# First layer of six experts by block products, turned rows copied by ScalarE, and one pool of banks, in a one-core graph and expert kernel

## The chip, the core and the metric

The kernel runs on one core of a Trainium2 chip. The metric is the device time of one execution in microseconds (us). Engines are named TensorE (PE in the profile; PEld is its weight loads), VectorE (DVE), ScalarE (ACT), GpSimd (POOL) and SyncE (SP). L1106 is line 1106 of the kernel before.

## The reference, cut to what matters

The input is 1250 rows (nodes) of 768 float32 values. A two-layer graph attention and a linear attention are added to it, and then a feed-forward part with eight experts, of which each row uses two:

```python
xt = layernorm(x)
scores, idx = top_k(xt @ Wg + bg, 2)
h = gelu(einsum('td,edh->eth', xt, W1) + b1[:, None, :])     # 768 -> 384, the first layer
y = einsum('eth,ehd->etd', h, W2) + b2[:, None, :]           # 384 -> 768, the second layer
out = x + sum over the two experts of a row of score * y
```

The kernel computes an expert only for rows that chose it. Everything is float32.

## The kernel before

The first part of the kernel (to about L1050) is the two attentions and, tile by tile of 125 rows, the norm and the routing: each tile's normalised rows and its eight gate values are written to a table in device memory, `xl_d` (L937 and L951), and a list `idx` of the rows that belong to each expert is built on VectorE with small products on TensorE (L958 to L1049). The last two of ten tiles are routed at 842 to 866 us.

Then the experts run. Each has three fixed tiles of 128 rows (`FIX`), and rows beyond that go to extra tiles (`other`, L1116), of which here one runs among the last expert's. For an expert:

- `gather` (L1060): three indirect loads on GpSimd's queue fetch rows by `idx` into `xg` (L1065, three buffers). Six transposes a tile on TensorE (L1074, "turns", into `px`) and two copies a tile on VectorE (L1075) make `xsT`, the turned rows: 768 values as 6 chunks of 128 partitions, by 384 rows. The gate values are copied at L1078.
- `inner` (L1081), the first layer: three blocks of 128 hidden values, each a sum of 6 products over the chunks (L1090, `ph`, 384 columns). ScalarE makes Gelu of each into `hT` (L1092). A float32 product runs as two passes, each counted as an instruction by the profile.
- `give` (L1095), for each of the three tiles: `gb`, the second bias by the gate value, on ScalarE (L1099); six products of 384 columns (L1106, `py`, two halves); `ys`, the result by the gate value plus `gb`, on VectorE (L1108, two halves, two buffers for three tiles); and a scatter that adds `ys` to rows of `out` from GpSimd's queue (L1110). Each scatter waits for the one before it, since both add to `out`.

The loop over experts 0 to 6 (L1160 to L1179) makes `inner` of expert e, `gather` of expert e+1, then the three `give` of expert e, and then issues from SyncE the second bias of expert e+2 (L1175) and both weight matrices of expert e+4 (`expert`, L748 and L750, ring of four buffers of 128x4608). The last expert (L1181 on) goes tile by tile together with the extra tile. A scheduler decides the order of each engine's instructions from dependences; an engine carries its own out in order. The eight banks of PSUM are shared out as two for turns (`x_p`), two for the first layer (`h_p`) and four for the second (`y_p`, L1056 to L1058). The large arrays `xnT` and `kept` of the attention part are no longer used when the experts run.

Of the kernel before, what the change touches and what calls it, by code (L numbers as in the profile page):

```python
# [27 lines left out]
F32 = mybir.dt.float32  # L28
# [5 lines left out]
AF = mybir.ActivationFunctionType  # L34
ALU = mybir.AluOpType
AX = mybir.AxisListType
PSUM = bass.MemoryType.PSUM
# [3 lines left out]
KC = D // 128  # L41
H1, C1, H2, C2 = 4, 192, 2, 96
HEADS, DH = 12, 64
NE, FF = 8, 384
FC = FF // 128
# [9 lines left out]
FIX = 3  # L55
# [5 lines left out]
def row_bcast(ap, parts):  # L61

    n = 1
    for s in ap.shape:
        n *= s
    return bass.AP(tensor=ap.tensor, offset=ap.offset, ap=[[0, parts], [1, n]])


@with_exitstack
def gps_block(ctx: ExitStack, tc: tile.TileContext, x, src, dst, norm_g, norm_b, W1, a_src1, a_dst1,  # L70
              b1, W2, a_src2, a_dst2, b2, Wu, bu, Wq, bq, Wk, bk, Wv, bv, Wo, bo, Wg, bg, fW1, fb1,
              fW2, fb2, out):
    nc = tc.nc
# [19 lines left out]
    kept = keep.tile([128, NT * H1 * CG], F32)  # L93
# [33 lines left out]
    xnT = big.tile([128, KC, N], F32)  # L127
# [4 lines left out]
    def bank(pool=None, name="mm"):  # L132
        return (pool or mm_p).tile([128, 512], F32, name=name)
# [37 lines left out]
    rows = fl.tile([KC, 128], F32)  # L171
# [36 lines left out]
    with tc.tile_pool(name="eps", bufs=4, space=PSUM) as eps_p:  # L208
# [4 lines left out]
        for k in (1, 0):  # L213
            nc.vector.memset(ends[k][:, T:], float(NO_NODE))
            for r0, r1 in blocks128:
# [5 lines left out]
                got = nc.scalar.copy(ends[k][:, r0:r1], pe[:, :nr])  # L221
# [78 lines left out]
    with tc.If(nc.values_load(odd[0:1, 0:1], min_val=0, max_val=1) > 0), ExitStack() as es:  # L300
# [9 lines left out]
        with tc.For_i(0, N, PT) as d0:  # L310
# [14 lines left out]
            with tc.For_i(0, TP, CH) as g:  # L325
                for u in range(CH):
                    at = bass.ds(g + u, 1)
                    count(ends[0][:, at], ends[1][:, at], False, u == CH - 1)
            A = cnt.tile([PT, N], F32)
            for i, (a, b) in enumerate(ACH):  # L330
                nc.scalar.copy(A[:, a:b], acc[:, i, :b - a])
            for g0 in range(0, NT, 4):
                n = min(4, NT - g0)
# [38 lines left out]
    with tc.tile_pool(name="ma_p", bufs=2, space=PSUM) as ma_p:  # L372
# [34 lines left out]
        ahead = {}  # L407
# [126 lines left out]
    def least(ss, H):  # L534
# [12 lines left out]
        return lo  # L547

    def attend(ss, sd, lo, wp, rb, gather):

        def across(cols, name, bufs, bias=0.0):
# [42 lines left out]
    with tc.tile_pool(name="wp", bufs=3) as wp, tc.tile_pool(name="rb", bufs=1) as rb:  # L594
        with tc.tile_pool(name="ag_p1", bufs=1, space=PSUM) as ag_p:
            for hd in range(H1):
# [10 lines left out]
                v = ag[:, :, :2 * CG].rearrange("p a (b c) -> p a b c", b=2)  # L607
# [8 lines left out]
        at = 2 * (C2 + 1)  # L616
# [22 lines left out]
    for t in range(NT):  # L639
# [3 lines left out]
        for k in range(2):  # L643
            half = slice(k * 384, (k + 1) * 384)
            for w in (Wk_sb, Wv_sb):
                ps = bank()
                for c in range(KC):
                    nc.tensor.matmul(ps[:PT, :384], xnT[:, c, t * PT:(t + 1) * PT], w[:, c, half],  # L648
                                     start=c == 0, stop=c == KC - 1)
# [10 lines left out]
            ps = bank()  # L660
            for c in range(3):
                nc.tensor.matmul(ps[:, c * 129:(c + 1) * 129],  # L662
                                 ky[:, (3 * k + c) * 128:(3 * k + c + 1) * 128], va[:, 3 * k + c],
                                 start=c == 0, stop=c == 2, skip_group_check=True)
            acc = kvacc[:, 3 * k:3 * k + 3]
            got = ps[:, :387].rearrange("p (b c) -> p b c", b=3)
# [25 lines left out]
    q3 = KC // 2  # L692
# [29 lines left out]
    for c in range(KC):  # L722
        ps = bank()
# [5 lines left out]
    for c in range(KC):  # L729
        for k in range(2):  # L730
            half = slice(k * 384, (k + 1) * 384)
            ps = bank()
# [12 lines left out]
    def expert(w1, w2, b2, b):  # L745

        t = wt.tile([128, KC, D], F32, name="w", bufs=4).rearrange("p c f -> p (c f)")
        nc.sync.dma_start(t[:, :KC * FF].rearrange("p (c f) -> p c f", c=KC),  # L748
                          w1.rearrange("(c p) f -> p c f", p=128))
        nc.sync.dma_start(t[:, KC * FF:].rearrange("p (c d) -> p c d", c=FC),  # L750
                          w2.rearrange("(c p) d -> p c d", p=128))
        if b2 is not None:
            nc.sync.dma_start(b, row_bcast(b2, 128))
        return t, b
# [5 lines left out]
    ring = []  # L760
# [7 lines left out]
    with ExitStack() as rs:  # L768
# [28 lines left out]
        for k in range(2):  # L797
            half = slice(k * 384, (k + 1) * 384)
            ps = bank()
# [195 lines left out]
        ahead = query(0)  # L995
        for p in range(NT // 2):
# [10 lines left out]
            if p + 1 < NT // 2:  # L1007
                ahead = query(p + 1)
# [44 lines left out]

    mix.close()
    sp = ctx.enter_context(tc.tile_pool(name="sp", bufs=2))
    x_p = ctx.enter_context(tc.tile_pool(name="x_p", bufs=2, space=PSUM))  # L1056
    h_p = ctx.enter_context(tc.tile_pool(name="h_p", bufs=2, space=PSUM))
    y_p = ctx.enter_context(tc.tile_pool(name="y_p", bufs=4, space=PSUM))  # L1058

    def gather(rows, e):  # L1060

        got = []
        for r in rows:
            xg = sp.tile([128, D + NE], F32, name="xg", bufs=3)
            nc.gpsimd.indirect_dma_start(xg, None, xl_d, bass.IndirectOffsetOnAxis(r, 0))  # L1065
            got.append(xg)
        xT = sp.tile([128, KC, FIX * 128], F32, name="xsT")
        gates = sp.tile([128, FIX], F32, name="gates")
        for j, xg in enumerate(got):
            for a in range(2):  # L1070
                px = x_p.tile([128, 512], F32, name="px")
                for c in range(3):
                    o = (3 * a + c) * 128
                    nc.tensor.transpose(px[:, c * 128:(c + 1) * 128], xg[:, o:o + 128], ident)  # L1074
                nc.vector.tensor_copy(xT[:, 3 * a:3 * a + 3, j * 128:(j + 1) * 128],  # L1075
                                      px[:, :384].rearrange("p (b n) -> p b n", b=3))
            at = slice(D + e, D + e + 1) if isinstance(e, int) else bass.ds(e + D, 1)
            nc.vector.tensor_copy(gates[:, j:j + 1], xg[:, at])  # L1078
        return xT, gates

    def inner(w, xT, bias, a=0, b=FIX, hT=None):  # L1081

        if hT is None:
            hT = sp.tile([128, FC, FIX * 128], F32, name="hT")
        n = slice(a * 128, b * 128)
        for f in range(FC):
            ph = h_p.tile([128, 512], F32, name="ph")
            for c in range(KC):
                o = c * FF + f * 128
                nc.tensor.matmul(ph[:, n], w[0][:, o:o + 128], xT[:, c, n], start=c == 0,  # L1090
                                 stop=c == KC - 1)
            nc.scalar.activation(hT[:, f, n], ph[:, n], AF.Gelu, bias=bias[:, f])  # L1092
        return hT

    def give(w, hT, j, rows, gates):  # L1095

        w, wb = w
        gb = sp.tile([128, D], F32, name="gb")
        nc.scalar.mul(gb, wb, gates)  # L1099
        ys = sp.tile([128, D], F32, name="ys")  # L1100
        for k in range(2):
            half = slice(k * 384, (k + 1) * 384)
            py = y_p.tile([128, 512], F32, name="py")
            for f in range(FC):
                o = KC * FF + f * D + k * 384
                nc.tensor.matmul(py[:, :384], hT[:, f, j * 128:(j + 1) * 128], w[:, o:o + 384],  # L1106
                                 start=f == 0, stop=f == FC - 1)
            nc.vector.scalar_tensor_tensor(ys[:, half], py[:, :384], gates, gb[:, half],  # L1108
                                           op0=ALU.mult, op1=ALU.add)
        nc.gpsimd.indirect_dma_start(out, bass.IndirectOffsetOnAxis(rows, 0), ys, None,  # L1110
                                     compute_op=ALU.add)

    def fixed(e):
        return [idx[:, v:v + 1] for v in range(e * NJ, e * NJ + FIX)]

    def other(k):  # L1116

        ve = nc.values_load(v_row[0:1, bass.ds(k, 1)], min_val=0, max_val=NV,
                            engines=[mybir.EngineType.DVE])
        ee = nc.values_load(e_row[0:1, bass.ds(k, 1)], min_val=0, max_val=NE - 1,  # L1120
                            engines=[mybir.EngineType.DVE, mybir.EngineType.SP])
        rows = sp.tile([128, 1], I32, name="rows")
        nc.vector.tensor_copy(rows, idx[:, bass.ds(ve, 1)])
        bias = sp.tile([128, FC, 1], F32, name="bias")
        nc.vector.tensor_copy(bias, fb1T[:, :, bass.ds(ee, 1)])
        w = expert(fW1[bass.ds(ee, 1)].rearrange("o d f -> (o d) f"),
                   fW2[bass.ds(ee, 1)].rearrange("o d f -> (o d) f"), fb2[bass.ds(ee, 1)],
                   sp.tile([128, D], F32, name="wb", bufs=1))
        return ee, rows, bias, w

    ahead = gather(fixed(0), 0)
# [19 lines left out]
    for vals, add, row in ((place, float(NV), v_row), (which, 0.0, e_row)):  # L1151
        pick = fp.tile([128, NE], F32, name="pick", bufs=2)
        nc.vector.tensor_mul(pick, vals, mine)
        one = fp.tile([128, 1], F32, name="one", bufs=2)
        nc.vector.tensor_reduce(one, pick, AX.X, ALU.add)
        pr = h_p.tile([128, 512], F32, name="ph")
        nc.tensor.transpose(pr[:1, :128], one, ident)
        nc.vector.tensor_scalar(row, pr[:1, :128], add, None, op0=ALU.add)

    for e in range(NE - 1):  # L1160
        xT, gates = ahead
        bias = fb1T[:, :, e:e + 1]
        if e:
            hT = inner(ring[e], xT, bias)
        else:
            hT = inner(ring[e], xT, bias, 0, 1)
            inner(ring[e], xT, bias, 1, FIX, hT)
        ahead = gather(fixed(e + 1), e + 1)
        if e == NE - 2:
            ee, more_rows, more_bias, more_w = first  # L1170
            more_xT, more_gates = gather([more_rows], ee)
        for j, rows in enumerate(fixed(e)):
            give(ring[e], hT, j, rows, gates[:, j:j + 1])
        if e + 2 < NE:
            nc.sync.dma_start(spare[e % 2], row_bcast(fb2[e + 2], 128))  # L1175
        if e + 4 < NE:
            ring.append(expert(fW1[e + 4], fW2[e + 4], None, spare[e % 2]))
        elif e + 4 == NE:
            first = other(0)  # L1179

    e = NE - 1  # L1181
    xT, gates = ahead
    bias = fb1T[:, :, e:e + 1]
    hT = inner(ring[e], xT, bias, 0, 1)
# [8 lines left out]
    with tc.If(count > 1):  # L1193
        with tc.For_i(1, count, 1) as k:
            ee, rows, bias, w = other(k)
            xT, gates = gather([rows], ee)
# [33 lines left out]
```

## Time and profile before

| what | us |
|---|---|
| median of three runs (lowest, highest) | 1097.52 (1096.05, 1099.54) |
| profiled execution: its own time | 1097.82 |
| its span | 1096.1 |
| TensorE busy, share of span | 1031.0, 94% |
| VectorE busy | 705.8, 64% |
| ScalarE busy | 359.9, 33% |
| granted TensorE clock, mean | 0.986 |
| first layer's start, experts 1 to 6 | 901.27, 926.50, 951.72, 976.95, 1002.17, 1027.40 |
| first layer's start, expert 7 | 1054.31 |

The profile is of one execution. A row of the timeline has the start, the duration, the engine, the line, the operation, what it writes and reads, how often it stands there without a break, and in brackets how long the engine stood idle before it and what ended that. A TensorE matmul's end is modelled, so starts are the better measure of a stretch. "Idle before" does not tell of a cost by itself; it tells what an engine waited for.

### The profile page before, as it was taken

The numbers are of one execution on the slowest core, as the hardware profiler recorded it, in microseconds if no ns is written. First come the engines' busy times: TensorE is split into PE (matmuls) and PEld (weight loads), VectorE is DVE, ScalarE is ACT, GpSimd is POOL, SyncE is SP. The second block draws the span as 40 slices with busy tenths as digits, with TensorE's granted clock in tenths as the row PEclk, the third lists the DMA queues.
The fourth block names the chain that finished last, engine by engine and source line by source line (L and its number), as shares of the span: only waits on it lengthen the run. The fifth ranks groups of instructions, "written<-read, shape, count | busy, mean of one in ns | idle before, by whom it ended". The sixth has DMA issues, their size and how long they took to land.

```text
span 1096.1 us, 12392 instructions
## 1 busy us (share of the span) xinstructions
PE 1031.0 (94%) x4630; PEld 701.6 (64%) x4630; DVE 705.8 (64%) x1460; ACT 359.9 (33%) x548; POOL 78.8 (7%) x106
## 2 busy tenths in 40 slices
PE   6999999999999999988999999999999499999996
PEld 5876666587878879544555555656665376666674
DVE  7866684697897957769687958686855522222321
ACT  4612226372728373283833121112110111111121
POOL 2000000000000000000001000000000122223321
PEclk9999999999999999999999999999999699999998
DMA  5060000000000002000035002021144847777534
GB/s 161 29 211 19 29 15 1 1 1 1 1 1 1 1 1 87 1 0 1 15 142 153 1 15 71 20 65 43 58 153 132 274 116 221 213 213 203 116 58 59
DMA packets 35412, 79.51 MB, mean 73 GB/s; under 512 B 7078, under 2 KB 15416, under 8 KB 35348
## 3 DMA queue, kind: packets, MB, share of 16 engines
q1 hardware_dynamic: 29588, 58.90, 16.8%
q0 software_dynamic: 5760, 19.78, 8.5%
q8 instruction: 37, 0.61, 0.2%
q14 instruction: 27, 0.22, 0.1%
HBM read 60.33 MB, written 18.34 MB: 72 GB/s over the span
## 4 chain that ended last, share of the span: by engine, by line
PE 73%; DVE 20%; DMA 2%; ACT 1%; issue 1%; POOL 0%; DVEq 0%; POOLq 0%; ACTq 0%
PE s L863 19%; PE mm L648 9%; PE ph L1090 9%; PE py L1106 8%; PE mm L477 8%; DVE scr L569 6%; DVE w L589 5%; DVE w L590 5%; PE ag L602 3%; PE mm L924 2%; PE ag L624 2%; PE ec L398 2%; PE mm L452 2%; PE px L1074 2%; PE rb L558 1%; PE mm L662 1%
## 5 line engine op out<-in xcount | busy, mean ns | idle before, releaser
L602 PE MATMUL ag<-kept,w 125*125 125x198 f32 x800 | 137.5, 333 | 5.1 <-DVE w L590 4.8
L602 PEld LDWEIGHTS ag<-kept,w 125*125 125x125 f32 x800 | 133.5, 188 | 9.0 <-DVE w L590 9.0
L1106 PE MATMUL py<-w,hT 128*128 128x384 f32 x300 | 100.9, 486 | 0.0
L1090 PE MATMUL ph<-xsT,w 128*128 128x384 f32 (+2 forms) x432 | 99.9, 390 | 0.0
L589 DVE TENSOR_TENSOR w<-v,w 125x1250 f32<-125x1250 f32 x60 | 86.3, 1453 | 6.0 <-ACT w L587 5.4
L648 PE MATMUL mm<-Wv_sb,xnT 128*125 128x384 f32 x240 | 85.6, 489 | 4.8 <-DVE kvacc L668 4.8
L1090 PEld LDWEIGHTS ph<-xsT,w 128*128 128x128 f32 x432 | 68.9, 191 | 30.3
L569 DVE CUSTOM_DVE_ANT_0 scr<-ss_row,mask 125x1250 bf16<-125x1250 f32 x60 | 87.2, 1453 | 1.6 <-ACT ss_row L560 1.2
L477 PE MATMUL mm<-Wg,xnT 128*125 128x400 f32 x240 | 87.7, 505 | 0.2 <-ACT xnT L367 0.2
L590 DVE SCALAR_TENSOR_TENSOR w<-w,AT 125x1250 f32<-125x1250 f32 x60 | 86.4, 1454 | 0.4
L588 ACT ACTIVATE v<-dn_row,sl 125x1250 f32<-125x1250 f32 x60 | 79.3, 1333 | 17.4 <-DVE w L589 16.9
L648 PE MATMUL mm<-Wk_sb,xnT 128*125 128x384 f32 x240 | 85.0, 487 | 0.0
L1108 DVE SCALAR_TENSOR_TENSOR ys<-py,gates,gb 128x384 f32<-128x384 f32 x50 | 30.3, 616 | 79.3 <-PE py L1106 54.7
L1106 PEld LDWEIGHTS py<-w,hT 128*128 128x128 f32 x300 | 55.1, 190 | 33.1
L1075 DVE COPY xsT<-px 128x384 f32<-128x384 f32 x50 | 25.8, 552 | 73.3 <-PE px L1074 73.3
L648 PEld LDWEIGHTS mm<-Wv_sb,xnT 128*125 128x125 f32 x240 | 42.5, 187 | 31.4 <-DVE kvacc L668 6.9
L477 PEld LDWEIGHTS mm<-Wg,xnT 128*125 128x125 f32 x240 | 42.5, 188 | 26.5 <-ACT xnT L367 0.9
L1099 ACT ACTIVATE gb<-spare,gates 128x768 f32<-128x768 f32 x24 | 22.4, 935 | 112.4 <-DVE ys L1108 94.8
L587 ACT ACTIVATE w<-up_row,s 125x1250 f32<-125x1250 f32 x40 | 53.2, 1331 | 17.7 <-PE ag L602 17.6
L648 PEld LDWEIGHTS mm<-Wk_sb,xnT 128*125 128x125 f32 x240 | 42.0, 187 | 22.7 <-issue 1.8
L863 PE MATMUL s<-w,xnT 128*125 128x384 f32 x150 | 55.4, 489 | 0.0
L863 PE MATMUL s<-w 128*125 128x384 f32 x150 | 53.9, 491 | 0.0
(328 smaller groups left out, 1515.1 us busy)
## 6 DMA issues: line engine op xcount, KB each, us to landing
w<-in_L_ffn_W_dram SPq DMA_DIRECT2D x18, 1152.0 KB
xt<-in_x_dram SPq DMA_DIRECT2D x20, 336.0 KB
out_dram<-xt SPq DMA_DIRECT2D x10, 336.0 KB
xl_d<-xl SPq DMA_DIRECT2D x10, 336.0 KB
spare<-in_L_ffn_b_dram SPq DMA_DIRECT2D x8, 384.0 KB
W_sb<-in_L_gnn_W_dram SPq DMA_DIRECT2D x1, 2304.0 KB
Wk_sb<-in_L_mix_Wk_dram SPq DMA_DIRECT2D x1, 2304.0 KB
Wv_sb<-in_L_mix_Wv_dram SPq DMA_DIRECT2D x1, 2304.0 KB
```

The lines of the kernel that those rows point to most:

```text
L477: nc.tensor.matmul(ps[:PT, :2 * (CG + 2)], xnT[:, c, t * PT:(t + 1) * PT], Wg1[:, c, 2 * k:2 * k + 2].rearrange("p h c -> p (h c)"), start ...
L569: nc.vector.tensor_tensor_reduce(scr, ss_row, mask[:, t], 1.0, 0.0, ALU.mult, ALU.max, top[:, t:t + 1])
L587: nc.scalar.activation(w, up_row, AF.Exp, bias=ss[:, st:st + 1])
L588: nc.scalar.activation(v, dn_row, AF.Exp, bias=sl[:, st:st + 1])
L589: nc.vector.tensor_tensor(w, v, w, op=ALU.max)
L590: nc.vector.scalar_tensor_tensor(w, w, 2.0, AT[:, st, :N], op0=ALU.min, op1=ALU.mult)
L602: nc.tensor.matmul(ag[:, t // 2, o:o + CG], w[:, t * PT:(t + 1) * PT], gw[:, st, hd], start=st == 0 and t % 2 == 0, stop=st == NT - 1, ski ...
L648: nc.tensor.matmul(ps[:PT, :384], xnT[:, c, t * PT:(t + 1) * PT], w[:, c, half], start=c == 0, stop=c == KC - 1)
L863: nc.tensor.matmul(ps, left[:, c], right[:, c], start=start and c == 0, stop=c == n - 1, skip_group_check=True)
L1090: nc.tensor.matmul(ph[:, n], w[0][:, o:o + 128], xT[:, c, n], start=c == 0, stop=c == KC - 1)
L1106: nc.tensor.matmul(py[:, :384], hT[:, f, j * 128:(j + 1) * 128], w[:, o:o + 384], start=f == 0, stop=f == FC - 1)
L1108: nc.vector.scalar_tensor_tensor(ys[:, half], py[:, :384], gates, gb[:, half], op0=ALU.mult, op1=ALU.add)
```

## The change

The first layer of experts 1 to 6 is computed as a product of two block matrices. The weights of the first layer are seen as 3 blocks of hidden values by 2 halves of the 768 inputs, the rows as 2 halves by 3 tiles, and each block as 3 chunks of 128x128. Plain multiplication takes 3x2x3 = 18 products of blocks; the change forms 15 from sums of blocks and adds the results up into the nine blocks of 128x128 of `hT`.

- 11 sums of weight blocks and 11 sums of row blocks per expert (`WAYS`; each 128x384, `make`), on VectorE, kept in the unused `xnT` and `kept`. The weight sums of expert e+1 are put between the products of expert e (`between`); the row sums of expert e+1 follow its `gather`, ahead of the three `give` of expert e.
- 15 products (`PRODUCTS`) of 3 matmuls of 128x128 each, in ten banks, five products adding onto a bank that already holds an earlier one.
- Out of the banks into `hT`: nine writes by ScalarE (copies and negated copies) and sixteen additions or subtractions by VectorE. Then ScalarE makes Gelu over `hT` in place, three times 128x384.
- `gather` for experts 1 to 7 copies the turned rows with ScalarE in place of VectorE.
- All banks of the expert part come from one pool of eight.

Experts 0 and 7 and the extra tile keep the plain `inner`. The diff, cut to its core:

```diff
+PRODUCTS = (
+    ("6", None, 1, 1, (1, "="), (2, "=-")),
+    ("10", None, 2, 4, (1, "+"), (3, "=-"), (7, "=")),
+    ("12", None, "12", 5, (8, "="), (9, "=")),
+    ("4", None, 5, "4", (8, "-"), (5, "=-")),
+    ("9", None, "9", "9", (4, "=-"), (3, "-")),
+    ("14", "6", "14", "14", (4, "+")),
+    ("13", None, "13", 3, (3, "+"), (6, "=")),
+    ("7", "12", "7", "7", (2, "+")),
...
-    x_p = ctx.enter_context(tc.tile_pool(name="x_p", bufs=2, space=PSUM))
-    h_p = ctx.enter_context(tc.tile_pool(name="h_p", bufs=2, space=PSUM))
-    y_p = ctx.enter_context(tc.tile_pool(name="y_p", bufs=4, space=PSUM))
+    e_p = ctx.enter_context(tc.tile_pool(name="e_p", bufs=8, space=PSUM))
...
+            def make(name=name, a=a, sign=sign, b=b):
+                op = nc.vector.tensor_add if sign > 0 else nc.vector.tensor_sub
+                op(got[name], got[a], got[b])
...
+    def inner15(A, B, bias, between):
+        hT = sp.tile([128, FC, FIX * 128], F32, name="hT")
+        C = [hT[:, i, j * 128:(j + 1) * 128] for i in range(3) for j in range(3)]
+        banks = {}
+        for name, onto, a, b, *uses in PRODUCTS:
+            ps = banks[name] = banks[onto] if onto else bank()
+            for c in range(q3):
+                nc.tensor.matmul(ps[:, :128], A[a][:, c], B[b][:, c], start=c == 0 and not onto,
+                                 stop=c == q3 - 1, skip_group_check=True)
+            for to, how in uses:
+                to = C[to - 1]
+                if how == "=":
+                    nc.scalar.copy(to, ps[:, :128])
+                elif how == "=-":
+                    nc.scalar.mul(to, ps[:, :128], -1.0)
+                elif how == "+":
+                    nc.vector.tensor_add(to, to, ps[:, :128])
+                else:
+                    nc.vector.tensor_sub(to, to, ps[:, :128])
+            if between:
+                between.pop(0)()
+        while between:
+            between.pop(0)()
+        for f in range(FC):
+            nc.scalar.activation(hT[:, f], hT[:, f], AF.Gelu, bias=bias[:, f])
+        return hT
...
+        between = []
+        if 0 < e < NE - 2:
+            A, between = weight_sums(ring[e + 1], e + 1)
         if e:
-            hT = inner(ring[e], xT, bias)
+            hT = inner15(now, B, bias, between)
+            now = A
         else:
             hT = inner(ring[e], xT, bias, 0, 1)
             inner(ring[e], xT, bias, 1, FIX, hT)
-        ahead = gather(fixed(e + 1), e + 1)
+        ahead = gather(fixed(e + 1), e + 1, nc.scalar.copy)
+        todo = []
+        if e < NE - 2:
+            B, todo = token_sums(ahead[0])
+        if e == 0:
+            now, between = weight_sums(ring[1], 1)
+        for make in todo:
+            make()
```

The weights, the indirect loads and the scatters are the same in number and size.

## The prediction

> **What bounds the kernel now.** I read the engines' totals first (TensorE 94% of the span), then the busy time of each engine between the starts of one expert's first layer and the next one's, then the timeline of one such stretch. The change touches experts 1 to 6, and these stretches say which wait ends last there:
>
> ```profile
> core 0: us, PE busy (x) PEld busy (x) DVE busy (x) ACT busy (x) POOL busy (x), PEclk, DMA share, GB/s
> 901.27:926.50 25.23, 25.23 (x92) 15.48 (x91) 6.91 (x15) 4.55 (x6) 7.67 (x6) 1.00 0.76 204
> 926.50:951.72 25.22, 25.22 (x91) 15.46 (x91) 6.91 (x15) 4.54 (x6) 7.70 (x6) 1.00 0.77 204
> ```
>
> The first column is the length of the stretch, the second TensorE's busy time: they are the same. An expert lasts 25.23 us because TensorE never stops; VectorE is busy for 6.91 and ScalarE for 4.55. So TensorE's saving shows only until something else takes 25 us. Two chains are already near. The timeline of one stretch:
>
> ```profile
> 926.34 11.77 PE L1090 MATMUL ph<-xsT,w 128*128 128x384 f32 x36
> 927.01 1.14 DVE L1108 SCALAR_TENSOR_TENSOR ys<-py,gates,gb 128x384 f32<-128x384 f32 x2 [3.73 <-DMA out_dram<-ys,idx]
> 927.68 1.59 POOL L1110 DMA_INDIRECT out_dram<-ys,idx  x1 [6.37 <-DVE ys L1108]
> ...
> 937.36 1.55 POOL L1110 DMA_INDIRECT out_dram<-ys,idx  x1 [8.09 <-DMA out_dram<-ys,idx]
> 937.95 0.82 PE L1074 MATMUL px<-ident,xg 128*128 128x128 f32 x6
> ...
> 944.02 0.62 DVE L1108 SCALAR_TENSOR_TENSOR ys<-py,gates,gb 128x384 f32<-128x384 f32 x1 [1.32 <-PE py L1106]
> 944.92 1.61 POOL L1110 DMA_INDIRECT out_dram<-ys,idx  x1 [2.14 <-DVE ys L1108]
> ...
> 951.75 0.37 SPq L748 DMA_DIRECT2D w<-in_L_ffn_W_dram  x1
> ...
> 952.21 1.14 DVE L1108 SCALAR_TENSOR_TENSOR ys<-py,gates,gb 128x384 f32<-128x384 f32 x2 [3.70 <-DMA out_dram<-ys,idx]
> ```
>
> The third tile's ys (952.21) uses the first tile's buffer (two buffers), so it waits until the first tile's scatter has landed: from the end of ys 0 (944.64) to ys 2 it is 7.57 us. Today VectorE merely idles there. And the scatters run one at a time: issues at 919.70, 927.68, 937.36, 944.92, that is 7.98, 9.68 and 7.56 apart. The list of waits over five experts has both:
>
> ```profile
> POOL out_dram L1110 <- DMA out_dram<-ys,idx: 40.0, 5, 8.1
> DVE ys L1108 <- DMA out_dram<-ys,idx: 18.8, 5, 3.9
> ```
>
> **TensorE's side.** First layer: 36 passes of 384 columns (18 products, two passes each) take from 926.34 to 937.95, 11.61 us, 322 ns a pass. The new one has 15 products of three 128x128 matmuls, 90 passes of 128 columns. Such passes are in the tail:
>
> ```profile
> 1066.05 4.18 PE L1090 MATMUL ph<-xsT,w 128*128 128x128 f32 x36
> 1070.07 1.13 PE L1106 MATMUL py<-w,hT 128*128 128x384 f32 x3
> ```
>
> 36 of them in 4.02 us (start to start): 112 ns, a third of 322, so nothing is lost to the narrow shape. 90 x 0.1117 = 10.05; the saving is 1.56 us an expert, 9.4 for six. Turns (18) and second layer (36 passes) stay: 25.23 - 1.56 = 23.67.
>
> **VectorE's side.** It loses six copies of xsT (3 pairs of 1.02 = 3.1 us) and gets, per expert, 22 sums of 128x384 and 16 additions of 128x128 out of PSUM. The nearest sums in the trace are 128x375:
>
> ```profile
> 702.70 0.55 DVE L856 TENSOR_TENSOR xnT<-xnT 128x375 f32<-128x375 f32 x1
> 703.17 0.54 DVE L857 TENSOR_TENSOR w<-w,xnT 128x375 f32<-128x375 f32 x1
> ...
> 704.21 0.55 DVE L1036 TENSOR_TENSOR kept<-kept,s 125x384 f32<-125x384 f32 x1
> 704.67 0.54 DVE L855 TENSOR_TENSOR zS<-qT 128x375 f32<-128x375 f32 x1
> 705.13 0.55 DVE L1018 TENSOR_TENSOR xt<-xt,kept 125x384 f32<-125x384 f32 x1
> ```
>
> Busy 0.55, but starts only 0.47 apart when the next does not read the last one's result, and 0.57 when it does (703.17 to 703.74). 22 x 0.465 = 10.2, with three dependent pairs 10.5. For the additions no row exists: 64-element operations start 0.15 apart (851.53, 851.68), 384-element ones 0.47, so 128 elements lie between; interpolated 0.21, taken as 0.20: 16 x 0.20 = 3.2 (bounds 2.4 and 7.5). VectorE then needs 10.5 + 3.2 + ys 3.4 + gates 0.3 = 17.4 of 23.67 us: enough if it never had to wait. But it takes its instructions in order, and in the built order of the changed program the three ys do not stand together. ys 2 of an expert stands ahead of all additions of the next one's products; then come 16 additions with 11 weight sums between and behind them; then 11 token sums; then ys 0 of the next. So the wait of ys 2 for the scatter, in which VectorE had nothing else to do, is now in series with all of that. Queued behind it are the additions, and on ScalarE gb of that tile (0.94) waits for ys 2 in front of the copies that empty the banks; TensorE's eighth product accumulates onto the third's bank, which ScalarE reads behind that gb. TensorE stands there. The loop, ys 0 to ys 0:
>
> end of ys 0 to ys 2: 7.57 as now if nothing else loads the queues; weight loads (951.75) now begin inside it, and a scatter beside such loads took 9.68 until the next could go. I take 8.3 (7.57 to 9.7). ys 2: 1.14; gates 0.27; additions 3.2; 22 sums 10.5; waits of the additions for ScalarE: gb 0.94, a negated copy 0.37 (as the 128x128 Gelu) and two plain ones at 0.27 (a copy of that size out of PSUM, L726) make 1.85, less 0.9 that VectorE has to do meanwhile, and two more negated copies behind it 0.8, so 1.7; wait for the first copy of turned rows, 0.5 (0 to 1.5); ys 0: 1.14. Sum 26.75, against 25.23 now: **+1.52**. It holds for experts 2 to 5 (expert 1 has its successor's weight sums done beforehand, expert 6 has none to make): 4 x 1.52 = +6.1. Expert 1 follows TensorE, -1.56. For expert 6 the loop is 11 sums shorter, but now scatters and the extra tile's gather bound it (26.91 today): -0.6 (-1.6 to +0.9).
>
> **ScalarE** gets nine bank copies (9 x 0.27 to 0.37), six copies of turned rows (0.47 each) and three Gelus from SBUF (0.58 each, as now): about 10 us of 25, so it is no bound by throughput; what hides it is that slack, and its order costs what stands above. One pool of eight banks costs nothing while the readers keep up, and is in the 1.7 where they do not. On the queues of SP and POOL gathers, scatters and loads keep their order, but for one weight load (848.21) that now goes ahead of the two writes of out's rows beside it, which nothing waits for then.
>
> **Ahead of the loop.** In the built order all 22 weight sums of experts 1 and 2 stand on VectorE among the routing of the last two token tiles: 4 ahead of the first one's normalised rows (850.68), 10 between that and the second one's (857.92), 8 between that and idx:
>
> ```profile
> 863.25 0.22 DVE L1049 SCALAR_TENSOR_TENSOR idx<-inv,free 128x80 int32<-128x80 f32 x1
> 865.48 1.06 POOL L1065 DMA_INDIRECT xg<-xl_d,idx  x1 [280.31 <-DVE e_row L1158]
> 871.95 2.46 PE L1074 MATMUL px<-ident,xg 128*128 128x128 f32 x9 [7.01 <-DMA xg<-xl_d,idx]
> ```
>
> TensorE idles 7 us for these gathers, so a later idx delays everything. The first 4 fall into idle time (2.72 before 846.14, 1.55 before 850.35). Ten take 4.7, less idle time 1.14 and 0.90: +2.7. Eight take 3.8, less about 0.8 of short gaps in that dependent chain: +3.0. idx is +5.7; between it and the gather there were 2.0, of which 1.7 are slack: the gather starts +4.0 later. Expert 0's turns now all stand ahead of its products, +0.5; weight loads that have gone further by then give some 0.5 back. I take **+4.0** (2 to 5.5; with a weight load later than its sum, more).
>
> **Sum:** 4.0 - 1.6 + 6.1 - 0.6 = +7.9. The profiled execution took 1097.82 (span 1096.1), 0.3 over the median 1097.52; so **1106**. 0.3% (3.3 us) is about what a measurement of this kernel can tell from no change.
>
> [...]
>
> **Rivals.**
> (a) *TensorE stays the bound.* If additions and sums go closer together than in my rows and the scatter lands by 7.57, with the waits for ScalarE hidden, the loop falls to 23.7 or less: 6 x -1.56 = -9.4, with the shift ahead +4.0: 1092.4 (1088.4 if the routing hides the sums too). For it: VectorE's work is 17.4. Against it: the order. It decides below 23.7, 3.1 less than my sum. 0.13.
> (b) *The loop is lighter.* At 7.57 for the scatter, 0.17 for an addition and 0.9 for ScalarE it is 24.7: 4.0 - 1.6 - 2.1 - 0.6 = -0.3, with half the shift ahead hidden lower yet; 1095 to 1101, about 1097.5. 0.17.
> (c) *The main case*, loop 25.8 to 28: 1101 to 1112, at 1106. 0.60.
> (d) *TensorE's clock falls in the stalls.* After 7.01 us idle it was granted 0.50 (871.95 to 873.50) and three turns took 0.92 for 0.33. If four stalls of 3 us did the same to the 48 passes behind them (5.4 us), up to 4 x 3 to 5.4 more: about 1120. [...] 0.07.
> (e) *The change does not do what it says*: TensorE's instruction list of the changed program has 45 matmuls in each of the six, so only the time could fail to move: 1097.5. 0.03.
>
> The range 1092 to 1113 takes in (a) with its shift, (b) and (c), and leaves out (d) and the lowest of (a). Faster by over 0.3%: (a), 0.13. Within: (e) and most of (b), 0.15. Slower: the rest, 0.72.
>
> **What would show it.** After: periods of about 23.7 for expert 1 and 26.5 to 27 for 2 to 5, with a TensorE gap of about 3 us behind the seventh product, released by ScalarE's copy; ys 2 waiting for the scatter with the additions behind it; idx some 5 us later; clock 1.00 in the loop. Equal periods near 23.7 with TensorE always busy would make this wrong, as would additions 0.14 or 0.4 apart, or a scatter that lands in 6.

## The result, and the profile after

The changed kernel took 1108.71 us (median of 6; 1105.64 to 1114.04) against 1098.74 for the kernel before (6 runs): ratio 1.0092, 95% interval 1.0068 to 1.0116. It is slower by 10 us; the forecast was 1106, or +7.9. The profiled execution took 1113.38 (span 1111.6, granted clock 0.975), one of the longer ones. Part of its length is older than the change: the same ScalarE instruction of the attention part (L904 before; called the mark below) starts at 790.57 before and at 795.66 after, though the program up to there is the same. So 5.1 of its 15.5 us are this execution's own, and 10.4 are the change's.

The stretches between first layers of the changed kernel, as shown for before. Columns: stretch, its length, busy time of each engine, granted clock, DMA share, GB/s:

```profile
910.79:935.09 24.30, 23.89 (x145) 18.93 (x144) 17.36 (x47) 8.51 (x21) 8.81 (x6) 1.00 0.77 200
935.09:961.10 26.01, 23.89 (x145) 18.93 (x144) 17.36 (x47) 8.51 (x21) 8.23 (x6) 1.00 0.73 200
961.10:986.47 25.37, 23.89 (x145) 18.93 (x144) 17.38 (x47) 8.51 (x21) 9.22 (x6) 1.00 0.76 203
986.47:1012.12 25.65, 23.89 (x145) 18.93 (x144) 17.35 (x47) 8.51 (x21) 8.02 (x6) 1.00 0.76 200
1012.12:1037.62 25.50, 23.89 (x145) 18.93 (x144) 12.82 (x36) 8.73 (x21) 7.95 (x6) 1.00 0.81 225
1037.62:1069.62 32.00, 27.59 (x152) 21.23 (x151) 9.58 (x28) 8.73 (x21) 6.05 (x5) 0.89 0.36 60
```

TensorE now has less to do than the stretch is long: something else ends it. Against 25.23 the first is 0.9 shorter, the next four together 1.6 longer, and expert 6 (26.91 before) is 5.1 longer. Ahead of them 910.79 stands against 901.27: +9.5, of which 5.1 were there at the mark already; the change's part is +4.4. With 0.2 at the end, 4.4 - 0.9 + 1.6 + 5.1 + 0.2 = 10.4.

One turn of the loop in the changed kernel's timeline:

```profile
950.57 1.03 DVE L1100 TENSOR_TENSOR xnT<-xsT 128x384 f32<-128x384 f32 x2 [0.35 <-ACT xsT L1157]
...
955.73 2.32 DVE L1190 SCALAR_TENSOR_TENSOR ys<-ps,gates,gb 128x384 f32<-128x384 f32 x4
...
957.14 1.61 POOL L1192 DMA_INDIRECT out_dram<-ys,idx  x1 [2.85 <-DVE ys L1190]
...
964.55 1.14 DVE L1190 SCALAR_TENSOR_TENSOR ys<-ps,gates,gb 128x384 f32<-128x384 f32 x2 [6.50 <-DMA out_dram<-ys,idx]
...
965.79 0.94 ACT L1181 ACTIVATE gb<-spare,gates 128x768 f32<-128x768 f32 x1 [3.37 <-DVE ys L1190]
...
966.79 0.59 ACT L1127 COPY hT<-ps 128x128 f32<-128x128 f32 x3
...
967.43 0.94 PE L1122 MATMUL ps<-xnT 128*128 128x128 f32 x6 [1.48 <-ACT hT L1127]
...
972.89 2.13 PE L1156 MATMUL ps<-ident,xg 128*128 128x128 f32 x18
```

The chain is the forecast's: ys 0 ends (956.87), its scatter lands, ys 2 starts 7.68 later (964.55), gb waits for it, ScalarE's bank copies for gb, TensorE's eighth product for the copies. TensorE's stall was 2.12, 1.48, 1.76 and 1.61 in experts 2 to 5; about 3 was expected. The granted clock stayed at 1.00.

Expert 6 is where most was lost. All 24 turns now stand ahead of its second layer, and the last six need the extra tile's rows:

```profile
1048.59 2.13 PE L1156 MATMUL ps<-ident,xg 128*128 128x128 f32 x18
1054.47 1.51 PE L1156 MATMUL ps<-ident,xg 128*128 128x128 f32 x6 [3.75 <-DMA xg<-xl_d,rows]
1055.78 14.00 PE L1188 MATMUL ps<-w,hT 128*128 128x384 f32 x36
```

The first 3.5 us after that wait by granted clock (the last three figures are clock, DMA share and GB/s):

```profile
1054.47:1058.00 3.53, 3.53 (x10) 2.62 (x11) 1.11 (x2) 0.00 (x0) 0.00 (x0) 0.50 0.02 5
```

TensorE idles 3.75 us and comes back at a granted clock of 0.50; the second layer then takes 13.84 (1055.78 to 1069.62), against 11.61 in the loop (949.49 to 961.10). Before, the turns stood between pieces of the second layer, and the idle time for these rows was 0.83.

Ahead of the loop:

```profile
874.39 0.22 DVE L1075 SCALAR_TENSOR_TENSOR idx<-inv,free 128x80 int32<-128x80 f32 x1
875.65 1.06 POOL L1147 DMA_INDIRECT xg<-xl_d,idx  x1 [285.49 <-DVE one L1237]
879.97 4.54 PE L1156 MATMUL ps<-ident,xg 128*128 128x128 f32 x18 [5.98 <-DMA xg<-xl_d,idx]
```

Less the 5.1 of the mark, idx is 6.0 later than before (863.25), the gather 5.1 (865.48), the first turn 2.9 (871.95), expert 1's first layer 4.4.

### The profile page after: what moved, and what is told of

Read it like the earlier page. It is cut to its first block, busy times and chain, and to the rows that moved or that the text cites. A ratio compares the mean times of both kernels' runs of the same rounds, so it can differ in the third digit from the quotient of the medians.

```text
span 1111.6 us, 13347 instructions
## 1 busy us (share of the span) xinstructions
PE 1032.4 (93%) x4954; PEld 730.7 (66%) x4954; DVE 765.6 (69%) x1646; ACT 386.6 (35%) x644; POOL 82.8 (7%) x106
## 4 chain that ended last, share of the span: by engine, by line
PE 64%; DVE 24%; DMA 5%; ACT 3%; issue 1%; POOL 0%; DVEq 0%; POOLq 0%; ACTq 0%; SPq 0%
PE s L889 18%; PE mm L674 9%; PE mm L503 7%; DVE scr L595 6%; DVE w L615 5%; DVE w L616 5%; PE ps L1188 4%; DMA out_dram<-ys,idx 3%; PE ag L628 3%; PE mm L950 2%; PE ag L650 2%; PE ps L1172 2%; PE ps L1122 2%; PE mm L478 2%; PE ec L424 2%; DVE xnT L1100 2%
## 5 line engine op out<-in xcount | busy, mean ns | idle before, releaser
L1188 PE MATMUL ps<-w,hT 128*128 128x384 f32 x300 | 100.6, 494 | 0.0
L1188 PEld LDWEIGHTS ps<-w,hT 128*128 128x128 f32 x300 | 57.4, 194 | 38.3 <-issue 2.1
L1190 DVE SCALAR_TENSOR_TENSOR ys<-ps,gates,gb 128x384 f32<-128x384 f32 x50 | 29.1, 612 | 76.8 <-PE ps L1188 36.4
L431 DVE TENSOR_TENSOR AT<-AT,ec 125x120 f32 x162 | 44.6, 275 | 11.5 <-PE ec L424 8.7
L650 PE MATMUL ag<-w,h 125*97 125x417 f32 (+1 forms) x120 | 46.6, 531 | 4.8 <-DVE w L616 4.8
L1192 POOL DMA_INDIRECT out_dram<-ys,idx x24 | 40.2, 1677 | 133.6 <-DVE ys L1190 82.2
```

What stands on the lines that cost most here:

```text
L431: nc.vector.tensor_add(here, here, ec[:, g])
L650: nc.tensor.matmul(ag[:, i, :b - a], h2[:, st, hd * (C2 + 1):(hd + 1) * (C2 + 1)], w[:, a:b], start=st == 0, stop=st == NT - 1)
```

## The experiments

**Theory 1**: the loop passes through VectorE's queue because ys 2 waits there for the scatter, and a third buffer breaks it. **Rival 2**: the scatters among themselves are the loop (now 8.1, 8.9 and 8.4 us apart). **Rival 3**: VectorE has too many small operations. The other two losses, ahead of the loop and in expert 6, were tried by themselves. All ratios are against the kernel before, on the same chip. Differences in us from the changed kernel are between medians of separate measurements, in which the kernel before stood between 1097.5 and 1099.3; they are good to a us or two.

### A third buffer for ys

```diff
-        ys = sp.tile([128, D], F32, name="ys")
+        ys = sp.tile([128, D], F32, name="ys", bufs=3)
```

> The changed kernel with three buffers for ys in place of two; nothing else. In the changed kernel the first layers of experts 2 to 5 start 25.4 to 26.0 us apart. Theory 1 (VectorE's in-order queue is the bound, since ys of the third tile waits 7.7 us for the first tile's scatter with the next expert's additions queued behind it): the wait goes, TensorE's stall after the seventh product goes, and the four periods fall to 23.7 to 24.3, some 5 to 7 us in all. Rival 2 (the chain of scatters, each of which waits for the one before: 8.1, 8.9 and 8.4 us apart now, sum 25.4): the periods stay within 0.3 us of 25.4 and the stall moves to the next tile of ys. Rival 3 (VectorE's own work of 38 small operations): the periods stay above 25 with VectorE busy and no scatter in its waits.

1100.78 us, ratio 1.0024 (1.0009 to 1.0040): 7.9 less than the changed kernel. All five stretches are 23.62 or 23.63, here the second and third:

```profile
928.69:952.32 23.63, 23.63 (x146) 18.86 (x145) 17.92 (x47) 8.72 (x21) 8.30 (x6) 1.00 0.82 219
952.32:975.94 23.62, 23.62 (x145) 18.85 (x144) 17.91 (x47) 8.72 (x21) 8.17 (x6) 1.00 0.81 221
```

TensorE is busy throughout, VectorE does no less than in the changed kernel (17.9 for 17.4), and the scatters fit into 23.6. Rivals 2 and 3 fall. It also measures TensorE's saving: 25.23 - 23.62 = 1.61 an expert. What remains over the kernel before is the start, and expert 6, which took 33.19.

### The sums behind idx

`routed` is the instruction that writes idx; `issue_after` keeps what VectorE gets within the block behind it.

```diff
-                op(got[name], got[a], got[b])
+                with tc.issue_after(routed.ins):
+                    op(got[name], got[a], got[b])
```

> The changed kernel with the sums put behind the instruction that writes idx on VectorE, so that none of the 22 weight sums of experts 1 and 2 stands among the routing; nothing else. Theory: from the last normalised rows on, idx comes some 5 to 6 us earlier, the gather of expert 0 starts about 4 us earlier, the sums fill VectorE's idle time while the gathers land, and the time falls by 3.5 to 5 us. Rival (the gather waits for the table's writes and weight loads anyway, or the sums are then late for expert 1): under 1.5 us, or a stall ahead of expert 1's third product.

1107.64 us, ratio 1.0082 (1.0065 to 1.0098): about 1 us less than the changed kernel, a miss. idx came early, at 861.68; then this, from VectorE and GpSimd:

```profile
861.68 0.22 DVE L1075 SCALAR_TENSOR_TENSOR idx<-inv,free 128x80 int32<-128x80 f32 x1
...
864.17 6.28 POOL L1149 DMA_INDIRECT xg<-xl_d,idx  x1 [280.10 <-DVE one L1239]
...
868.97 0.54 DVE L1102 TENSOR_TENSOR xnT<-w,kept 128x384 f32<-128x384 f32 x1
870.75 0.97 POOL L1149 DMA_INDIRECT xg<-xl_d,idx  x1 [0.30 <-issue]
```

The first gather's issue took 6.28 in place of 1.06: it ended (870.45) 0.94 after VectorE's run of sums paused (869.51), and 0.94 to 1.06 is what such an issue takes undisturbed. What was won at idx was lost at the issue: expert 1's first layer starts at 904.74 with the mark at 789.87, still 4.2 later than before. This led to a further run.

### The sums behind expert 0's copies

`turned[0]` is VectorE's last copy of expert 0's turned rows.

```diff
+                with tc.issue_after(turned[0].ins):
+                    op(got[name], got[a], got[b])
```

> The changed kernel with all sums put behind the last copy of expert 0's turned rows on VectorE, so that the 22 weight sums of experts 1 and 2 stand neither among the routing nor beside the issue of expert 0's gathers (in the run before with the sums right behind idx, idx came early but the issue of the first gather took 6.28 us on GpSimd in place of 1.06). Theory: the issue takes 1.1 us again, the first turn comes some 3 us earlier than in the changed kernel, expert 1's first layer 3.5 to 4.5 us earlier against the same point of the attention part, and the time falls by as much. Rival (the gathers wait for the table or for weight loads, not for VectorE): under 1.5 us.

1103.34 us, ratio 1.0049 (1.0027 to 1.0072): 5.4 less than the changed kernel. The issue is short again:

```profile
865.89 1.06 POOL L1150 DMA_INDIRECT xg<-xl_d,idx  x1 [278.69 <-DVE one L1241]
```

Expert 1's first layer starts at 902.14, with the mark at 792.12 (790.57 before): 0.7 earlier than before, where the changed kernel was 4.4 later. So the whole shift ahead of the loop came from where the 22 sums stood.

### The extra tile's gather behind the second tile

```diff
         for j, rows in enumerate(fixed(e)):
             give(ring[e], hT, j, rows, gates[:, j:j + 1])
+            if e == NE - 2 and j == 1:
+                ee, more_rows, more_bias, more_w = first
+                more_xT, more_gates = gather([more_rows], ee, name="xg_more", bufs=1)
```

> The changed kernel with the extra tile's gather put after the second tile's second layer of expert 6, with a buffer of its own for the rows; nothing else. In the changed kernel expert 6 lasts 32.0 us, with TensorE idle for 3.75 us for that gather and a granted clock of 0.50 after it. Theory: both go, the period falls to 25 to 27, the time by 5 to 7 us. Rival (the scatters or VectorE bound that expert): the period stays above 28.5, the time falls by under 3.5 us.

1104.79 us, ratio 1.0045 (1.0027 to 1.0062): 3.9 less than the changed kernel, for the 5 to 7 expected; expert 6 lasts 25.89 for 32.00, as expected. The order and the buffer of its own were not tried apart.

### The three edits together, two ways

With the sums behind idx, and a third buffer for gb:

> All three edits together, and three buffers for gb. If the three losses are separate and each is as the theories say, experts 1 to 6 follow TensorE at 23.7 to 24.3 and the time is 1089 to 1095, below the kernel before. Rival 2 (the chain of scatters bounds the loop at 25.4): 1098 to 1101. Rival 3 (VectorE's work): 1097 to 1100 with VectorE never idle in the loop.

1092.96 us, ratio 0.9934 (0.9911 to 0.9957), below the kernel before: stretches of 23.62, expert 6 24.28, but the first gather's issue takes 5.71 here too, and the shift ahead of the loop stays at 4.5 (907.45, mark 792.25).

With the sums behind the copies:

> The changed kernel with three buffers for ys, the extra tile's gather behind the second tile's second layer, and the sums behind the last copy of expert 0's turned rows. Theory: experts 1 to 5 at 23.62, expert 6 at 24.3, no shift ahead of them beyond 0.5: 1087 to 1090, 3 to 6 us below the run with the sums right behind idx. Rival (the shift ahead of the experts stays): 1092 to 1094.

1086.07 us, ratio 0.9889 (0.9866 to 0.9912). It is the fastest version. Stretches of experts 1, 3 and 6:

```profile
900.88:924.50 23.62, 23.62 (x145) 18.86 (x144) 17.91 (x47) 8.74 (x21) 8.22 (x6) 1.00 0.78 211
948.13:971.75 23.62, 23.62 (x145) 18.86 (x144) 17.90 (x47) 8.74 (x21) 8.16 (x6) 1.00 0.81 222
1019.00:1043.29 24.29, 24.29 (x152) 19.47 (x151) 9.31 (x27) 8.73 (x21) 5.42 (x4) 1.00 0.44 68
```

TensorE never stops from expert 1 to 6. Five times 1.61 and 26.91 - 24.29 = 2.6 make 10.7; the span is 1085.4 for 1096.1.

### The copies of turned rows back on VectorE

```diff
-        ahead = gather(fixed(e + 1), e + 1, nc.scalar.copy)
+        ahead = gather(fixed(e + 1), e + 1)
```

> The changed kernel with the copies of turned rows back on VectorE, 6 x 0.51 = 3.1 us for each expert. If VectorE's queue with the scatter's wait in it is the loop that bounds experts 2 to 5, nearly all of it is added to each period, less the wait for ScalarE's first copy: 27.5 to 28.7 in place of 25.4 to 26.0, some 8 to 12 us in all. Rival (the scatters among themselves or the banks bound the loop, and VectorE has room): the periods stay within 0.5 us.

1120.94 us, ratio 1.0198 (1.0149 to 1.0246): 12 more than the changed kernel. Stretches of experts 1 to 5: 25.83, 26.97, 33.48, 27.36, 27.43, against 24.30, 26.01, 25.37, 25.65, 25.50. The total is what theory 1 expects, but its parts are not the copies alone:

```profile
921.97 5.64 POOL L1147 DMA_INDIRECT xg<-xl_d,idx  x1 [0.30 <-PE ps L1188]
...
948.89 5.73 POOL L1147 DMA_INDIRECT xg<-xl_d,idx  x1 [0.30 <-PE ps L1188]
...
967.32 1.14 DVE L1190 SCALAR_TENSOR_TENSOR ys<-ps,gates,gb 128x384 f32<-128x384 f32 x2 [10.05 <-DMA out_dram<-ys,idx]
...
970.19 1.65 PE L1122 MATMUL ps<-xnT 128*128 128x128 f32 x6 [7.24 <-ACT hT L1127]
...
998.28 0.96 PE L1122 MATMUL ps<-xnT,kept 128*128 128x128 f32 x6 [1.84 <-ACT hT L1127]
999.30:1001.30 2.00, 2.00 (x11) 2.00 (x11) 2.00 (x8) 0.27 (x1) 0.00 (x0) 0.50 1.10 304
```

Beside the row sums two gather issues took 5.64 and 5.73 for 1.06; the second ended (954.62) 0.86 after the last of them (953.76). Behind it the scatter of ys 0 went late (956.18), ys 2 waited for it until 967.32, and TensorE stood for 7.24, after which the granted clock was 0.50. In experts 4 and 5 TensorE stood for 1.84 and 1.91, little more than the 1.76 and 1.61 of the changed kernel; there the granted clock fell to 0.50 behind the stall (999.30 to 1001.30), and TensorE was busy for 25.52 in place of 23.89. So this run does not show that the copies' own 3.1 us lengthen the loop; the third buffer above and the row sums below bear that theory without it.

In the fastest version, with the wait for the scatter out of the queue, the same edit:

> The fastest version with the copies of turned rows back on VectorE (3.1 us of work an expert). With the scatter's wait out of its queue VectorE has room: about 18 + 3 of 23.6 us. If room decides, periods stay at 23.6 to 23.9 and the time within 2 us of 1086; if the queue's order alone costs, 24.5 or more and 1091 or more.

1092.40 us, ratio 0.9937 (0.9912 to 0.9962): 6 more than the fastest version, so the "within 2 us" is missed. Four of five stretches are 23.62 or 23.63; the second is 29.24:

```profile
915.72 5.15 POOL L1196 DMA_INDIRECT out_dram<-ys,idx  x1 [7.30 <-DVE xnT L1101]
...
921.17 1.03 POOL L1150 DMA_INDIRECT xg<-xl_d,idx  x1 [0.30 <-DVE ys L1194]
...
931.35 0.15 DVE L1163 COPY gates<-xg 128x1 f32<-128x1 f32 x1 [2.07 <-DMA xg<-xl_d,idx]
```

VectorE has room by its sums, but beside its row sums (914.19 to 919.34) the issue of a scatter took 5.15 for 1.6 (1.55 to 1.94 at the same place in the four turns after); the gathers queued behind it on GpSimd come late, the gate values wait for them, and behind these on VectorE the additions. TensorE stood for 3.72 and came back at a granted clock of 0.63 (932.58 to 934.00), then 0.50 (934.00 to 936.00).

### Parts of the change alone

One pool and ScalarE's copies, without block products and sums:

> The change without its block products and sums: the plain first layer everywhere, one pool of eight banks, turned rows of experts 1 to 7 copied by ScalarE. Theory (the extra tile's turns stand ahead of expert 6's second layer because the pool lets the scheduler take all turns at once): experts 1 to 5 at 25.2 as in the kernel before, expert 6 longer than the 26.9 of before by 3 to 6 us, the time 1101 to 1104. Rival (the products and their sums do it): expert 6 at 26.9, the time as before.

1101.09 us, ratio 1.0031 (1.0016 to 1.0045). Experts 1 to 5 take 25.19, expert 6 takes 30.17 for 26.91:

```profile
1039.23 2.13 PE L1156 MATMUL ps<-ident,xg 128*128 128x128 f32 x18
1044.13 1.51 PE L1156 MATMUL ps<-ident,xg 128*128 128x128 f32 x6 [2.77 <-DMA xg<-xl_d,rows]
```

The pool alone, with the copies on VectorE:

> The kernel with one pool of eight banks alone: plain first layer everywhere and turned rows copied by VectorE, as before. If the pool lets all 24 turns of expert 6 go ahead of its second layer, TensorE waits there for the extra tile's rows: expert 6 some 30 us for 26.9, experts 1 to 5 at 25.2, the time 1100 to 1103. Rival (ScalarE's copies are what moves the turns): expert 6 at 26.9 and the time as before.

1100.14 us, ratio 1.0015 (0.9994 to 1.0037): on the time alone unclear. The trace shows the same order, an idle time of 2.97 and 30.54 for expert 6 (1025.90 to 1056.44). So the pool is what moves the turns: with two banks for turns the scheduler put pieces of the second layer between them, with eight it did not.

A third buffer for ys in the kernel before:

> The kernel before with three buffers for ys, nothing else. VectorE waits for the scatter there too, but TensorE bounds the loop: the wait goes and nothing is gained, periods 25.2, the time within 1 us of before. Rival (the wait costs something there already): 2 us or more faster.

1098.07 us, ratio 0.9988 (0.9968 to 1.0007), stretches of 25.22 and 25.23 still. The wait was there, and cost nothing as long as TensorE was the bound.

### The row sums in the scatter's wait

`given` is the second half of the second tile's ys.

```diff
-        for make in todo:
-            make()
...
+            if j == 1:
+                with tc.issue_after(given.ins):
+                    for make in todo:
+                        make()
```

> The changed kernel with two buffers for ys as it is, but the eleven row sums put behind the second tile's ys on VectorE, into the wait of the third tile's ys for the scatter. Expert 5 of the changed kernel, which has no weight sums to make, still lasted 25.50, so the weight sums lie beside TensorE's last eight products, and the loop that bounds it is: scatter 7.6, ys, gb and ScalarE's copies, eight products 5.4, turns and their copies, row sums 5.2, ys. Theory: without the row sums the loop is some 20.3 and experts 2 to 5 follow TensorE at 23.6 to 23.9 with two buffers. Rival (the scatter's wait with two buffers costs its 2 us whatever stands where): 25 or more.

1098.34 us, ratio 1.0018 (0.9998 to 1.0038): 10 less than the changed kernel, with two buffers. Stretches 23.63, 23.62, 23.72, 24.05, 23.63. So the wait need not go; it is enough that work of the loop is done within it. The expectation's account of the loop holds: without 5.2 us of row sums in it, it is no longer the bound.

## Why the prediction was right or wrong

The direction, the place of the new bound and the time (1106 for 1108.7, within 1092 to 1113) were right; two terms of the sum were wrong by 4.5 and 5.7 us and of opposite sign: it is luck that the sum is closer than its terms. Case (c), which has this time, supposed a loop of 25.8 to 28; it was 25.63 on average, between (b)'s 24.7 and that. With expert 6 as forecast, an estimate from the stretches above is about 1103.

- **TensorE's side**: 1.56 an expert forecast, 1.61 measured (third buffer). Right.
- **VectorE's pieces**: additions at 0.20 were measured so (945.08, three in 0.67 with the last one's 0.27), and the sums, busy for 0.55 each, start 0.47 apart (953.39, 953.86). By that spacing the eleven row sums take 5.2.
- **The loop, "Sum 26.75 ... 4 x 1.52 = +6.1"**: the mechanism is right (third buffer, row sums), the size is not: +1.6. The failed term is "22 sums 10.5" in series with the rest. Only the eleven row sums are; the weight sums lie between additions that wait for TensorE's last eight products anyway, and VectorE still waits 0.35 for ScalarE's copies ahead of the row sums (950.57). Expert 5 shows it: no weight sums (36 operations for 47, VectorE busy 12.82 for 17.36) and yet 25.50. The loop runs from the scatter over ys 2, gb and ScalarE's copies to TensorE's eight products and turns, the row sums, ys 0. The scatter took 7.68 and 7.94 in the two turns from 956.87, for the 8.3 taken. The text also had the weight sums one expert too late.
- **Expert 1**: -1.56 forecast, -0.9 measured, with a first short stall of 0.41.
- **Expert 6, "-0.6 (-1.6 to +0.9)"**: this step failed, +5.1. The 24 turns ahead of the second layer stood in the built order, and the text gave "one pool of eight banks" no price of its own. The pool alone shows the order and 3 to 4 us of it.
- **Ahead of the loop, +4.0**: 4.4 measured, and the sums behind the copies take all of it away. idx +6.0 for 5.7, the gather +5.1 for 4.0. The rows then landed faster (issue to first turn 4.32, 6.47 before), and expert 0 took 1.5 more for 0.5, its 18 turns all at a clock of 0.50.
- **Rival (d), the clock**: not in the loop of the profiled execution, where the stalls were shorter than expected (1.48 to 2.12, clock 1.00); it came where nobody had put it, behind the extra tile's wait. That the loop was spared need not hold in every execution: with the sums behind expert 0's copies a stall of 2.00 (933.22) was followed by products 1.28 apart (934.86, 936.14) in place of 0.67, the spacing that stands beside a granted 0.50 with the copies on VectorE (971.64, 972.92), and that stretch lasted 27.51.

What is not settled: why the rows of expert 0 landed 2 us faster (a weight load stood behind the table's writes in both), why some issues on GpSimd are held up by VectorE's sums and most are not, and why executions differ by up to 6 us ahead of all that was changed (the mark lies between 789.3 and 795.7 in these runs).

## What to carry to other kernels

A wait that cost nothing while another engine was the bound became part of the loop here once work was queued behind it (a third buffer for ys took 7.9 us off the changed kernel and, at a ratio of 0.9988, nothing that can be told off the kernel before): before adding work to an in-order queue, look for waits in it, and give them a buffer or put the new work in front of the wait. Work that is moved to an idle engine is free only where it stands in no chain; look at what a scheduler does with it, here sums that it took up among the routing (idx 6.0 later). And a change of a pool is a change of order: with fewer limits on buffers the scheduler ran TensorE's in-order queue ahead into a wait that the limits had kept it from (2.97 us idle in place of 0.83 with the pool alone).

## What the runs showed of the hardware

- **A few of GpSimd's issues of an indirect DMA were held up by a run of VectorE sums, and most were not.** A gather's issue took 1.06 with VectorE idle (865.89, sums behind the copies). Beside 128x384 sums from SBUF, 0.47 apart, one took 6.28, 5.71, 5.64, 5.73 and, in the fastest version with VectorE's copies, 6.06 (890.47); a scatter's, 1.6 alone, took 2.87 in the changed kernel (974.16) and 5.15. With the sums behind idx (6.28, 5.71) the first gather was held up, with the sums behind the copies (1.06) it was not, so there the sums are the cause. But beside row sums of the same size and spacing the changed kernel's fifteen gathers from 925.94 to 1030.41 took 1.02 to 1.25, those at 927.28 and 953.23 1.05 and 1.06. No run here tells which sums hold up an issue and which do not.
- **The length of a stall did not tell whether TensorE's clock fell.** Stalls of 0.83, 1.76, 2.12, 2.73 (extra tile's gather moved, 993.23), 3.07 (copies on VectorE, 939.07) and 3.92 (sums behind idx, 1049.45) left the granted clock at 1.00 (behind 2.73 and 3.07 the products start 0.67 apart). Stalls of 1.84 and 1.91 (copies on VectorE), 2.00 (sums behind the copies), 2.77, 2.97 and 3.75 were followed by 0.50 (for 1.91 and 2.00 this is read from products 1.28 apart). No length of a stall parts the two groups: 1.84 stands in the second, and 3.92 in the first.

An undisturbed gather beside two of the row sums (changed kernel), then the longest of these stalls that left the clock at 1.00 (sums behind idx) and the 4 us behind it; a short one that did not is shown with the copies on VectorE:

```profile
953.23 1.06 POOL L1147 DMA_INDIRECT xg<-xl_d,idx  x1 [0.30 <-issue]
953.39 0.55 DVE L1100 TENSOR_TENSOR kept<-xnT,xsT 128x384 f32<-128x384 f32 x1
953.86 0.55 DVE L1100 TENSOR_TENSOR kept<-xsT,xnT 128x384 f32<-128x384 f32 x1
...
1049.45 0.85 PE L1158 MATMUL ps<-ident,xg 128*128 128x128 f32 x6 [3.92 <-DMA xg<-xl_d,rows]
1049.45:1053.45 4.00, 4.00 (x17) 2.67 (x18) 1.64 (x3) 0.00 (x0) 0.00 (x0) 1.00 0.02 4
```
